# Rotary queries and keys kept transposed through DRAM, instead of turned by matrix products for each unit

## The chip, the cores and the metric

The kernel runs on one core of one Trainium2 chip. The metric is the device time of one execution in microseconds, the median of several runs. The core has TensorE (PE, matrix products), VectorE (DVE), ScalarE (ACT), GpSimd (POOL) and SyncE (SP), which issues most DMAs. Each engine takes its instructions in the order in which they were written.

## The reference

One layer on x of 4096 tokens by 256: attention, layer norm, a gated feed-forward network (FFN) of width 1024, layer norm. Cut to the part that the change touches:

```python
proj = quant4(x) @ ternary_weight(Wqkv_w).T + Wqkv_b
q = proj.reshape(B, N, h, dk).transpose(0, 2, 1, 3)   # 16 heads of 16 columns
k = proj.reshape(B, h, N, dk)                         # heads are blocks of 256 tokens
v = proj.reshape(B, h, N, dk)
q, k = (rotary(q, N), rotary(k, N))                   # even and odd columns turned by cos, sin
ql, kl = (q @ U, k @ U)
att = jnp.einsum('bhnr,bhmr->bhnm', ql, kl) / math.sqrt(dk)
y = jax.nn.softmax(att, axis=-1) @ v
```

`quant4` rounds each token to integers from -8 to 7 times the token's maximum over 7; `ternary_weight` makes the weight -1, 0 or 1 times a scale per input column of the product. Queries take a head from a column group of 16; keys and values take a head from 256 tokens, and a key's 4096 positions are (token of the 256) x (column group of 16).

## The kernel before

**Units.** The attention is 64 units: 8 pairs of heads times 8 blocks of 512 queries. A unit has 32 steps, a step is one loop turn. In a step, `largest` (L470, L478) multiplies 128 queries of the unit by 512 keys for two heads, each into a PSUM bank `ps`, and VectorE takes the maximum of each row; `weights` (L516, L524), 40 steps behind (`LAG`), forms the transposed scores minus the maximum by two products for each head and ScalarE takes the exponential; `values` (L538), 4 steps further behind and once in two steps, multiplies them by the values. The banks `ps` are three, shared by `largest` and everything else that TensorE makes beside it.

**Operands.** TensorE wants `kT` (128 x 4096) and `qT` (128 x 512) with the inner dimension on the partitions: 64 rows per head, being the keys' high part, low part, high, low, and the queries' high, high, low, low (a product of float32 numbers by parts). `gmat` is U times U transposed, over the root of 16, in blocks; only the keys are multiplied by it.

**Where they come from.** `projection_steps` makes, for each block of 512 tokens, the projection in token order (`v_all`). `key_steps` rotates a pair's keys in token order on GpSimd, turns them by eight products with the identity (L362), multiplies them by `gmat` (L368), splits them in parts (L377, L378), doubles these (L383) and turns the result by 32 products with the identity in eight groups (L394), each evacuated by ScalarE. It runs once per pair, over four units of the pair before. `query_steps` does the same for each unit's queries: six rotations on GpSimd (L330 to L335), two instructions that split (L432, L433), four products that turn them (L440), one evacuation (L447).

**The order** is written out by hand: `at(step, f)` puts f in the list of a step, and a step's list runs in the order of entry before that step's `weights`. All engines follow that order. Blocks 1 to 7 are projected at steps 32(b - 2) + 17 and on (block 1 in unit 0). The lists of the blocks are filled before the lists of the units.

**The maxima's way.** At the end of a unit VectorE reduces the maxima (L483). At the next unit's step 1 ScalarE rounds them (L490) and GpSimd subtracts (L491, `m_parts`); at step 3 VectorE transposes them (L497, `m_turned`); SP stores them to DRAM and loads them as `m_rows` (L502, L505); `weights` needs these from step 8 on.

Of the kernel before, what the change touches and what calls it, by code (L numbers as in the profile page):

```python
# [9 lines left out]
F32 = mybir.dt.float32  # L10
# [8 lines left out]
P = 128  # L19
# [18 lines left out]
def attn_ffn_kernel(  # L38
# [17 lines left out]
    cos: bass.AP,  # L56
    sin: bass.AP,
# [23 lines left out]
    y_dram = [dram.tile([QB, D], F32, name=f"y_dram{b}") for b in range(NQB)]  # L81
    flag = const.tile([1, 1], I32, name="flag")
# [9 lines left out]
    def ternary(w, wabs, neg, bank, sgn, alpha):  # L92

# [7 lines left out]
        nc.vector.tensor_scalar(alpha, ps[:, :D], 1.0 / D, None, ALU.mult)  # L101
# [7 lines left out]
        nc.vector.scalar_tensor_tensor(sgn, w, th, neg, ALU.is_ge, ALU.subtract)  # L109

    def linear_steps(src, sgn, bank, eng, evacuate):


        held = {}

        def measure():

            ma = stat.tile([P, BT], F32, name="ma")
            nc.vector.tensor_reduce(ma, src, AX.X, ALU.max, apply_absolute_value=True)  # L119
            nc.vector.tensor_scalar(ma, ma, 1e-6, None, ALU.max)  # L120
            held["ma7"] = stat.tile([P, BT], F32, name="ma7")
            nc.vector.tensor_scalar(held["ma7"], ma, 1.0 / 7.0, None, ALU.mult)
            held["rec"] = stat.tile([P, BT], F32, name="rec")
            nc.vector.reciprocal(held["rec"], ma)

        def integers():
            t = quantp.tile([P, BT, D], F32, name="qtmp")
            rec = held["rec"].unsqueeze(2).broadcast_to([P, BT, D])
            eng.tensor_tensor(t, src, rec, ALU.mult)
            eng.tensor_scalar(t, t, 7.0, ROUND, ALU.mult, ALU.add)  # L130
            eng.tensor_scalar(t, t, ROUND, -8.0, ALU.subtract, ALU.max)
            held["q"] = quantp.tile([P, BT, D], BF16, name="qint")
            eng.tensor_scalar(held["q"], t, 7.0, None, ALU.min)
# [9 lines left out]
        def project(i0):  # L143
            ps = bank([P, 512], F32)
            for i in range(i0, i0 + 2):
                for k in range(2):
                    nc.tensor.matmul(  # L147
                        ps[:, ts(i - i0, D)],
                        lhsT=held["qT"][:, k, i, :],
                        rhs=sgn[:, k, :],  # L150
                        start=(k == 0),
                        stop=(k == 1),
                    )
            for i in range(i0, i0 + 2):
                evacuate(i, ps[:, ts(i - i0, D)], held["ma7"][:, i : i + 1])

        return measure, integers, transposed, lambda: project(0), lambda: project(2)


# [51 lines left out]
    def front_steps(b, bank):  # L211
# [10 lines left out]
        first, *others = linear_steps(yb, sgn_o, bank, nc.vector, evacuate)  # L222

        def integers():
            first()
            others[0]()
# [4 lines left out]
            *others[1:],  # L231
# [6 lines left out]
    with ExitStack() as actx:  # L238
# [7 lines left out]
        cos_q = big.tile([P, NT, HALF], F32, name="cos_q")  # L246
        sin_q = big.tile([P, NT, HALF], F32, name="sin_q")
        cos_k = big.tile([P, 2, H, HALF], F32, name="cos_k")
        sin_k = big.tile([P, 2, H, HALF], F32, name="sin_k")
# [19 lines left out]

        def set_up():  # L270
# [7 lines left out]
            ut, ut8, mask = small[:32, :DK], small[:32, P : 2 * P], small[:, 2 * P : 3 * P]  # L278
            nc.sync.dma_start(out=ut, in_=uT)
            nc.sync.dma_start(out=mask, in_=blockmask)  # L280
            tables = ((cos, cos_q, cos_k), (sin, sin_q, sin_k))
            for src, _, tk in tables:
                nc.sync.dma_start(out=tk, in_=src.rearrange("(a p c) f -> p a c f", a=2, p=P))
            nc.sync.dma_start(out=bias_bc, in_=bqkv.partition_broadcast(P))
            for src, tq, _ in tables:
                nc.sync.dma_start(out=tq, in_=src.rearrange("(t p) f -> p t f", p=P))
# [3 lines left out]
            ternary(tw[0], wabs[:, 0], neg[:, 0], bank1, sgn_qkv, alpha_qkv)  # L290
            nc.gpsimd.tensor_copy(
                ut8.rearrange("r (j e) -> r j e", e=DK), ut.unsqueeze(1).broadcast_to([32, 8, DK])
            )
            psg = bank1([P, 512], F32)
            nc.tensor.matmul(psg[:, :P], lhsT=ut8, rhs=ut8, start=True, stop=True)
            nc.vector.tensor_tensor(gmat, psg[:, :P], mask, ALU.mult)

            def later():

                nc.gpsimd.memset(minus.bitcast(F32), -1.0)  # L300
                nc.gpsimd.memset(m_parts.bitcast(F32), 0.0)
                for i in range(2):
                    nc.gpsimd.memset(m_rows[i].bitcast(F32), 0.0)
                nc.gpsimd.memset(v_chunk[:, :, :, DK : DK + 1], 1.0)
                nc.gpsimd.memset(v_all[:, :, H * (DK + 1) :], 0.0)
                ternary(tw[1], wabs[:, 1], neg[:, 1], bank1, sgn_o, alpha_o)

            return later

        def projection_steps(b, eng):  # L310


            def evacuate(i, ps, ma7):
                v = v_chunk[:, b * BT + i, :, :DK]
                nc.vector.scalar_tensor_tensor(
                    v,
                    ps.rearrange("p (c e) -> p c e", e=DK),
                    ma7,
                    alpha_qkv.rearrange("p (c e) -> p c e", e=DK),
                    ALU.mult,  # L320
                    ALU.mult,
                )
                eng.tensor_tensor(v, v, bias_bc.rearrange("p (c e) -> p c e", e=DK), ALU.add)

            return linear_steps(x_bufs[b % 2], sgn_qkv, bank1, eng, evacuate)

        def rotate(lo, hi, even, odd, c, s, shape, key, eng=nc.gpsimd):

            t = [rot.tile(shape, F32, name=f"{key}{i}") for i in range(4)]
            eng.tensor_tensor(t[0], even, c, ALU.mult)  # L330
            eng.tensor_tensor(t[1], odd, s, ALU.mult)
            eng.tensor_tensor(lo, t[0], t[1], ALU.subtract)
            eng.tensor_tensor(t[2], even, s, ALU.mult)
            eng.tensor_tensor(t[3], odd, c, ALU.mult)
            eng.tensor_tensor(hi, t[2], t[3], ALU.add)  # L335

        def key_steps(pair, kT, eng=nc.gpsimd):


            kr = kprep.tile([P, 2, H, 2, DK], F32, name="kr")  # L340
            krT = kprep.tile([P, 2 * H * 2 * DK], F32, name="krT")
            kn = kprep.tile([P, 2 * H, 2, 4, DK], F32R, name="kn")

            def rotate_keys(j):
                src = v_chunk[:, 2 * (2 * pair + j) : 2 * (2 * pair + j) + 2]
                rotate(
                    kr[:, :, :, j, :HALF],
                    kr[:, :, :, j, HALF:],
                    src[:, :, :, 0:DK:2],
                    src[:, :, :, 1:DK:2],  # L350
                    cos_k,
                    sin_k,
                    [P, 2, H, HALF],
                    "rk",
                    eng,
                )

            def transpose_raw(i):
                ps = ps_1.tile([P, 512], F32, name="ps1")
                flat = kr.rearrange("p a c j e -> p (a c j e)")  # L360
                for k in range(4):
# [591 lines left out]
```

## Time and profile before

| what | value |
|---|---|
| median of 3 runs | 3701.32 us (3701.28 to 3702.39) |
| the profiled execution | 3702.95 us |
| its span | 3701.1 us, 62137 instructions |
| granted TensorE clock, mean | 0.986 |
| first L478 (VectorE) | 39.4 us |
| L483 of unit 0, 7, 63 | 96.1, 430.5, 2951.4 us |
| last `weights` product, FFN from | 3003 us, 3008 us |

The chain of waits follows the work that ended last back from the end, and gives each engine and line its share. A row of the timeline has start and length in us, engine, line, operation, tiles and shapes, and in brackets how long the engine was idle before it and for whom. A row of the groups has the busy time, the mean of one in ns, and the idle time before them. A row of the stretches has the busy time of PE, PEld, DVE, ACT and POOL with the count of instructions, the granted clock, the DMA share and GB/s.

### The profile page before, as it was taken

Reading aid. Unit: us, or ns where it says so; the run is one execution under the profiler, and the core shown is the slowest. Engines: PE = TensorE matmul, PEld = TensorE weight load, DVE = VectorE, ACT = ScalarE, POOL = GpSimd, SP = SyncE. Lnnn points to the kernel's source line nnn. Section 1 sums busy time; section 2 is a strip of 40 time slices with the busy share of each in tenths; the row PEclk is TensorE's granted clock in tenths of the full one; section 3 lists DMA queues with packets and bytes.
Section 4 is the critical chain, followed back from the end, with each engine's and each line's share of the span. In section 5 each row is a group of like instructions: output and inputs, shape, how many; then the busy total and the mean of one; then the engine's idle time right before and its main releaser. Section 6 shows DMA issues by size and latency. Waiting matters only on the chain.

```text
span 3701.1 us, 62137 instructions
## 1 busy us (share of the span) xinstructions
PE 3627.2 (98%) x24395; PEld 2055.8 (56%) x24395; DVE 3066.4 (83%) x5638; ACT 2384.5 (64%) x2782; POOL 525.0 (14%) x968
## 2 busy tenths in 40 slices
PE   6999999999999999999999999999999979999998
PEld 3454555555555555555555555555555448888887
DVE  6998999999999999998999899989999925555544
ACT  1567777777777777777777777777777753333333
POOL 3342112111211121121112111210111010000000
PEclk7999999999999999999999999999999989999999
DMA  1000000011000000000000000000121020001000
GB/s 37 15 24 14 20 20 20 20 23 23 20 20 20 20 20 20 21 20 20 20 20 20 20 20 20 20 14 14 38 64 26 21 82 6 18 18 35 18 6 13
DMA packets 247038, 84.52 MB, mean 23 GB/s; under 512 B 188880, under 2 KB 241360, under 8 KB 246736
## 3 DMA queue, kind: packets, MB, share of 16 engines
q1 hardware_dynamic: 242912, 68.93, 8.3%
q0 software_dynamic: 3824, 11.54, 1.0%
q8 instruction: 193, 3.16, 0.4%
q14 instruction: 109, 0.89, 0.1%
HBM read 54.22 MB, written 26.21 MB: 22 GB/s over the span
## 4 chain that ended last, share of the span: by engine, by line
PE 97%; DVE 2%; ACT 0%; DMA 0%; POOL 0%; issue 0%; SPq 0%; DVEq 0%; ACTq 0%; POOLq 0%
PE av L538 27%; PE sc L516 27%; PE ps L470 21%; PE ps_mm L785 17%; PE ps L394 1%; PE ps L440 1%; DVE mx L478 1%; PE ps L368 1%; PE ps L147 0%; DMA y_raw<-yt 0%; PE ps L362 0%; DVE ma L119 0%; PE ps_mm L830 0%; ACT pr L524 0%; PE ps_mm L147 0%
## 5 line engine op out<-in xcount | busy, mean ns | idle before, releaser
L478 DVE TENSOR_REDUCE mx<-ps 128x1 f32<-128x512 f32 x4096 | 2560.4, 684 | 210.7 <-PE ps L470 165.6
L524 ACT ACTIVATE pr<-sc 128x1024 f32<-128x1024 f32 x2048 | 2006.6, 1023 | 773.2 <-PE sc L516 759.4
L470 PEld LDWEIGHTS ps<-kT,qT 64*128 64x128 f32 x4096 | 557.7, 185 | 968.8 <-DVE mx L478 747.4
L538 PE MATMUL av<-pr,v_all 128*32 128x512 f32 x8192 | 1092.8, 605 | 0.0
L470 PE MATMUL ps<-kT,qT 64*128 64x512 f32 x4096 | 1051.7, 471 | 10.9 <-DVE mx L478 8.6
L516 PE MATMUL sc<-m_rows,minus 64*128 64x512 f32 x4096 | 842.7, 404 | 4.0 <-ACT pr L524 3.6
L516 PE MATMUL sc<-qT,kT 64*128 64x512 f32 x4096 | 817.7, 390 | 0.0
L516 PEld LDWEIGHTS sc<-m_rows,minus 64*128 64x128 f32 x4096 | 394.4, 185 | 89.1 <-ACT pr L524 38.3
L516 PEld LDWEIGHTS sc<-qT,kT 64*128 64x128 f32 x4096 | 395.7, 185 | 75.8
L538 PEld LDWEIGHTS av<-pr,v_all 128*32 128x32 f32 x8192 | 161.7, 108 | 267.3 <-issue 266.6
L818 ACT ACTIVATE gate<-ps_mm,sc_hs 128x512 f32<-128x512 f32 x128 | 88.3, 690 | 312.6 <-PE ps_mm L785 269.5
L491 POOL TENSOR_TENSOR m_parts<-m,m_parts 128x8 fp32r<-128x8 f32 x64 | 13.0, 203 | 1849.3 <-ACT m_parts L490 1849.3
L767 DVE CAST h<-gate 128x512 fp32r<-128x512 f32 x128 | 54.4, 425 | 223.1 <-ACT gate L818 223.0
L769 DVE TENSOR_TENSOR h<-gate,h 128x512 fp32r<-128x512 f32 x192 | 132.3, 689 | 5.1
L559 DVE STREAM_TRANSPOSE yt<-ya 128x64 f32<-128x64 f32 x512 | 119.0, 234 | 18.8 <-ACT ya L553 18.8
L785 PE MATMUL ps_mm<-h,h1a 128*128 128x512 f32 x512 | 128.9, 394 | 0.0
L785 PE MATMUL ps_mm<-h,h2a 128*128 128x512 f32 x512 | 127.2, 390 | 0.0
L785 PE MATMUL ps_mm<-h,h1b 128*128 128x512 f32 x512 | 126.5, 389 | 0.0
L785 PE MATMUL ps_mm<-h,h2b 128*128 128x512 f32 x512 | 126.5, 389 | 0.0
L810 DVE SCALAR_TENSOR_TENSOR gate<-ps_mm,sc_s,gate 128x512 f32<-128x512 f32 x64 | 48.0, 750 | 83.2 <-ACT gate L808 58.0
L785 PEld LDWEIGHTS ps_mm<-h,h1b 128*128 128x128 f32 x512 | 96.1, 188 | 20.1
L785 PEld LDWEIGHTS ps_mm<-h,h2b 128*128 128x128 f32 x512 | 96.1, 188 | 20.0
(147 smaller groups left out, 1954.1 us busy)
## 6 DMA issues: line engine op xcount, KB each, us to landing
y_raw<-yt SPq DMA_DIRECT2D x256, 64.0 KB
y<-y_raw SPq DMA_DIRECT2D x64, 256.0 KB
xs<-in_x SPq DMA_DIRECT2D x16, 512.0 KB
y_dram<-yu SPq DMA_DIRECT2D x64, 64.0 KB
xs<-in_h1T SPq DMA_DIRECT2D x8, 512.0 KB
xs<-in_h2T SPq DMA_DIRECT2D x8, 512.0 KB
yb<-y_dram SPq DMA_DIRECT2D x8, 512.0 KB
out<-xs SPq DMA_DIRECT2D x8, 512.0 KB
```

What stands on the lines that cost most here:

```text
L368: nc.tensor.matmul(ps[:, ts(k, P)], lhsT=krT[:, ts(4 * i + k, P)], rhs=gmat, start=True, stop=True,)
L470: nc.tensor.matmul(ps[j], lhsT=qTs[u][rows, ts(qt, P)], rhs=kTs[u // NQB][rows, ts(ck, 512)], start=True, stop=True,)
L478: nc.vector.tensor_reduce(mxs[u][:, qt, j, ck : ck + 1], ps[j], AX.X, ALU.max)
L516: nc.tensor.matmul(ps[:, j, :], lhsT=minus[rows, :] if first else kTs[u // NQB][rows, ts(kt, P)], rhs=m_rows[u % 2][rows, :] if first else ...
L524: nc.scalar.activation(pr, ps, AF.Exp)
L538: nc.tensor.matmul(avs[u][strip : strip + 32, :], lhsT=v_all[:, 2 * (2 * pair + j) + a, c * (DK + 1) : c * (DK + 1) + 32], rhs=probs[s + k ...
L559: nc.vector.transpose(yts[u][:, ts(i, 64)], yas[u][:, ts(i, 64)])
L767: eng(dst[:, k, 0, :], g)
L769: nc.vector.tensor_tensor(dst[:, k, 1, :], g, dst[:, k, 0, :].bitcast(F32), ALU.subtract)
L785: nc.tensor.matmul(ps, lhsT=sb[:, ks, ts(o, P)] if split else wo[:, k, :], rhs=src[:, k, i, :], start=(k == 0 and i == 0), stop=(k == n - ...
L810: nc.vector.scalar_tensor_tensor(g, pb, scales["s2"][:, o : o + 1], gate, ALU.mult, ALU.mult)
L818: nc.scalar.activation(g, ps, AF.Gelu, scale=scales[sc][:, o : o + 1])
```

## The change

Queries and keys are no longer taken from the projection in token order. For each block of 512 tokens the projection is made a second time, transposed: the weight's even columns and then its odd columns are the stationary operand, so that row (column group, frequency) x token comes out (`even_odd`). There the rotation is a plain product with tables `csq` (for queries) and `csk` (for keys) of the same layout. The token's scale, which was a scalar per partition, is now a row: `start_scales` stores the maxima to DRAM and loads them to all partitions. `queries` rotates, splits in high and low and `store_queries` writes them to `q_dram`. `rotate_keys` rotates with the other table, `regroup_keys` moves halves of 64 partitions by DMA so that a head's 16 rows stand together, `times_g` multiplies by `gmat` (two products of 512 columns) and splits, `store_keys` writes to `k_dram`. A unit's `qT` is loaded by four DMAs (`load_queries`), a pair's `kT` by eight (`load_keys`). `key_steps`, `query_steps` and `rotate` are gone, with L362, L368, L394 and L440. The positions of the keys are in another order (`values` takes c and a the other way round).

Block b, from 1 to 7, is now worked wholly within unit b - 1 and the start of unit b, since its queries are the ones of unit b. For blocks from 1 on GpSimd does the even and odd rows' scale and bias, the rotations, the parts of the queries and the natural projection's scale and bias, and ScalarE empties the banks; for block 0, before the first step, VectorE and ScalarE do most of it. The zero and one fills and the output weight's signs, which stood at step 8, stand before the first step. Two scalar operations of the rounding have another form. The diff, cut:

```diff
-            nc.vector.tensor_scalar(ma, ma, 1e-6, None, ALU.max)
+            eng.tensor_scalar(ma, ma, 1e-6, None, ALU.max)
...
-            eng.tensor_scalar(t, t, ROUND, -8.0, ALU.subtract, ALU.max)
+            eng.tensor_scalar(t, t, 1.0, -ROUND, ALU.mult, ALU.add)
...
-            eng.tensor_scalar(held["q"], t, 7.0, None, ALU.min)
+            eng.tensor_scalar(held["q"], t, 7.0, -8.0, ALU.min, ALU.max)
...
+        def start_scales(b, held):
+            row = ma_dram[b % 2]
+            nc.sync.dma_start(out=row.rearrange("t p -> p t"), in_=held["ma7"])
+            held["scale"] = rot.tile([P, QB], F32, name="scale")
+            nc.sync.dma_start(out=held["scale"],
+                in_=row.rearrange("t p -> (t p)").unsqueeze(0).broadcast_to([P, QB]))
+        def even_odd(b, held, o):
...
+            for k in range(2):
+                nc.tensor.matmul(ps, lhsT=sgn_qkv[:, k, o::2],
+                    rhs=held["qT"][:, k].rearrange("p t q -> p (t q)"),
+                    start=(k == 0), stop=(k == 1))
+            if b:
+                nc.scalar.activation(x, ps, AF.Copy, scale=alpha2[:, o : o + 1])
+                nc.gpsimd.tensor_tensor(x, x, held["scale"], ALU.mult)
+                nc.gpsimd.tensor_scalar(x, x, bias2_sb[:, o : o + 1], None, ALU.add)
...
+        def queries(b, held):
+            t, u = two("rot")
+            copies, second = (nc.gpsimd.tensor_copy, nc.gpsimd) if b else (nc.scalar.copy, nc.vector)
+            c, s = (held["cs"][:, i].unsqueeze(1).broadcast_to([P, 2, QB]) for i in range(2))
+            nc.gpsimd.tensor_tensor(t, held["eo"], c, ALU.mult)
+            nc.gpsimd.tensor_tensor(u, held["eo"], s, ALU.mult)
+            nc.gpsimd.tensor_tensor(t[:, 0], t[:, 0], u[:, 1], ALU.subtract)
+            second.tensor_tensor(u[:, 0], u[:, 0], t[:, 1], ALU.add)
...
+            for h, x, eng in ((0, t[:, 0], nc.gpsimd), (1, u[:, 0], second)):
+                copies(q[:, h, 0], x)
+                eng.tensor_tensor(q[:, h, 1], x, q[:, h, 0].bitcast(F32), ALU.subtract)
...
+        def rotate_keys(b, held, eng):
...
+            eng.tensor_tensor(t.rearrange(by_head, j=2), eo, c, ALU.mult)
+            eng.tensor_tensor(u.rearrange(by_head, j=2), eo, s, ALU.mult)
+            eng.tensor_tensor(t[:, 0], t[:, 0], u[:, 1], ALU.subtract)
+            eng.tensor_tensor(u[:, 0], u[:, 0], t[:, 1], ALU.add)
...
+        def times_g(b, held, x):
+            ps = bank1([P, QB], F32)
+            nc.tensor.matmul(ps, lhsT=gmat, rhs=held["keys"][:, x], start=True, stop=True)
+            high, low = (held["parts"][:, 2 + x, i] for i in range(2))
+            nc.scalar.copy(high, ps)
+            nc.vector.tensor_tensor(low, ps, high.bitcast(F32), ALU.subtract)
...
+        def load_queries(u, queue=nc.sync):
+            pair, qb = divmod(u, NQB)
+            qTs[u] = qpool.tile([P, QB], F32R, name="qT", bufs=3)
+            for j in range(2):
+                for i in range(2):
+                    row = 64 * j + 2 * DK * i
+                    queue.dma_start(out=qTs[u][row : row + 2 * DK, :].bitcast(F32),
+                        in_=q_dram[qb][2 * pair + j, i].unsqueeze(0).broadcast_to([2, DK, QB]))
...
             for b in range(1, NQB):
-                steps = projection_steps(b, nc.gpsimd)
-                first = NKT * (b - 2) + 16 if b > 1 else 0
+                first = NKT * (b - 1)
...
+                    for i in range(BT):
+                        at(first - 9 + 2 * i, lambda i=i, f=biggest: f(i))
...
+                def prepare(b=b, h=h, measure=measure, integers=integers):
+                    measure()
+                    start_scales(b, h)
+                    h["cs"] = load_tables(b)
+                    integers()
+                if b > 1:
+                    at(first + 1, prepare)
...
+                at(first + 10, transposed)
+                for o in range(2):
+                    at(first + 12 + 2 * o, lambda b=b, h=h, o=o: even_odd(b, h, o))
+                at(first + 15, lambda b=b, h=h: queries(b, h))
+                at(first + 23, lambda b=b, h=h: store_queries(b, h))
+                for i in range(2):
+                    at(first + 16 + 2 * i, lambda b=b, h=h, i=i: natural(b, h, 2 * i))
+                at(first + 22, lambda b=b, h=h: rotate_keys(b, h, nc.gpsimd))
+                at(first + 34, lambda h=h: regroup_keys(h))
+                for x in range(2):
+                    at(first + 39 + 2 * x, lambda b=b, h=h, x=x: times_g(b, h, x))
+                    at(first + 43, lambda b=b, h=h, x=x: store_keys(b, h, x))
...
-                        steps = key_steps(pair + 1, kTs[pair + 1])
-                        for i, f in enumerate(steps):
-                            at(NKT * u + 40 + 6 * i, f)
+                        for i in range(4):
+                            at(NKT * u + 40 + 8 * i,
+                                lambda i=i: load_keys(pair + 1, kTs[pair + 1], i // 2, i % 2))
...
-                    at(NKT * (u - 1) + 26 if u else 0, transposed)
...
-                    at(NKT * (u - 1) + (18 if u == 1 else 6), start_queries)
+                    at(NKT * (u - 1) + (25 if u < NQB else 14), lambda u=u: load_queries(u))
```

## The prediction

> **What bounds the kernel now.** I read the page's busy times and its chain of waits first.
>
> ```profile
> PE 3627.2 (98%) x24395; PEld 2055.8 (56%) x24395; DVE 3066.4 (83%) x5638; ACT 2384.5 (64%) x2782; POOL 525.0 (14%) x968
> ...
> PE av L538 27%; PE sc L516 27%; PE ps L470 21%; PE ps_mm L785 17%; PE ps L394 1%; PE ps L440 1%; DVE mx L478 1%; PE ps L368 1%; PE ps L147 0%; DMA y_raw<-yt 0%; PE ps L362 0%; DVE ma L119 0%; PE ps_mm L830 0%; ACT pr L524 0%; PE ps_mm L147 0%
> ```
>
> TensorE is the chain. The lines that the change deletes (L394, L440, L362; L368 is replaced by as much) are in it, so they are paid for. By how much, the timeline of VectorE in the last units tells: L483 runs once per unit, and the last unit has no query turn (L440) for a successor.
>
> ```profile
> 2864.12 0.22 DVE L483 TENSOR_REDUCE m<-mx 128x8 f32<-128x64 f32 x1
> ...
> 2908.09 0.22 DVE L483 TENSOR_REDUCE m<-mx 128x8 f32<-128x64 f32 x1
> ...
> 2951.39 0.22 DVE L483 TENSOR_REDUCE m<-mx 128x8 f32<-128x64 f32 x1
> ```
>
> 43.97 us with L440, 43.30 without: 0.67 us a unit. The timeline of all engines in unit 8 says the same: `av` bursts are 2.70 us apart, but 3.38 across L440.
>
> ```profile
> 462.82 1.06 PE L538 MATMUL av<-pr,v_all 128*32 128x512 f32 x8
> ...
> 464.71 0.66 PE L440 MATMUL ps<-identr,qq 128*128 128x128 f32 x4
> ...
> 466.20 1.06 PE L538 MATMUL av<-pr,v_all 128*32 128x512 f32 x8
> ```
>
> The table by stretches (PE, PEld, DVE, ACT, POOL busy) shows a plain unit and a cycle of eight with one key preparation:
>
> ```profile
> 460.10:504.20 44.10, 44.07 (x325) 22.25 (x324) 41.50 (x76) 33.27 (x40) 3.95 (x11) 1.00 0.08 15
> ...
> 697.70:1059.10 361.40, 361.34 (x2654) 184.11 (x2654) 333.93 (x602) 267.93 (x309) 55.81 (x110) 1.00 0.10 21
> ```
>
> 361.4 - 8 x 44.03 = 9.2 us per pair for L362, L368 and L394; from the gaps between bursts, 2 x 0.68 + 2 x 1.17 + 8 x 0.68 = 9.1. VectorE (41.5 of 44.1) is next, 1.8 us short of the 43.3 that remain: it does not take over in a plain unit.
>
> **Steady part, units 8 to 63.** 56 x 0.67 = 37.5 us and six key preparations (pairs 2 to 7), 6 x 9.2 = 55.2 us, go: **-92.7 us**. What comes in their place is on SP and the DMA engines: 4 query loads per unit and 8 key loads (256 KB each) per pair. They are issued 18 or more steps (24 us) before use; w1's 1 MB took 6.6 us to land. The last key pair is issued 3 steps before `m_turned`'s store; that hop takes 2.0 us (rows below), and `m_rows` is read 5 steps (6.8 us) after it, so some 2.8 us cover it. Without cover: at most about 3 us x 7.
>
> **The first eight units pay.** Before, L483 of units 0 and 7 are at 96.1 and 430.5: 334.4 us for seven units, 31.3 above 7 x 43.3. Now six of those units (1 to 6) each do a whole block on GpSimd. What its instructions cost, by groups and by the timeline of GpSimd:
>
> ```profile
> L620 POOL TENSOR_TENSOR xs<-xs,wround 128x1024 f32<-128x1024 f32 x22 | 52.4, 2383 | 1.8
> ...
> L330 POOL TENSOR_TENSOR rk<-v_all,cos_k 128x256 f32<-128x256 f32 x14 | 10.4, 746 | 0.0
> ...
> L383 POOL CAST kn<-kn 128x1024 fp32r<-128x1024 f32 x14 | 14.5, 1042 | 0.1
> ```
> ```profile
> 266.41 1.89 POOL L129 TENSOR_TENSOR qtmp<-xs,rec 128x1024 f32<-128x1024 f32 x1 [13.39 <-DVE rec L124]
> 268.39 1.05 POOL L130 TENSOR_SCALAR qtmp<-qtmp 128x1024 f32<-128x1024 f32 x1
> 269.52 3.64 POOL L131 TENSOR_SCALAR qtmp<-qtmp 128x1024 f32<-128x1024 f32 x1
> 273.24 2.77 POOL L133 TENSOR_SCALAR qint<-qtmp 128x1024 bf16<-128x1024 f32 x1
> ```
>
> A two-input operation: 2.38 us at 1024, 0.74 at 256, so 1.29 at 512. Multiply-then-add (L130) is fast, the forms with subtract, max or min are slow. Per block:
> - integers: 1.89 + 1.05 + 1.05 (the subtraction is now a multiply-add) + the new min-then-max. That form is not in the trace: 2.77 (one operation) to 6.4 (3.64 + 2.77); I take 3.64, the two-operation row. Sum 7.6.
> - even and odd rows: 2 x (1.29 + adding a bias by pointer). The latter, at 512: 0.5 (half of L130) to 1.8 (half of L131); I take 1.4, half of the single operation L133. Sum 5.4.
> - queries: 4 products and sums, 2 x 2.38 + 2 x 1.29, 2 casts of 0.6, 2 subtractions of 1.29: 11.1.
> - natural: 4 x (0.74 + 0.68) = 5.7; rotated keys: 2 x 2.38 + 2 x 1.29 = 7.3.
>
> 37.1 us, with the small ones (limits, `m_parts`, y, yu) 38.6, of a unit of 44: it fits, but in a poor order. `prepare` (first + 1) and `largest_parts` stand at the same step and `prepare` was entered first; GpSimd runs the four integer operations, then the small L491. Before, this chain was, by the timeline:
>
> ```profile
> 475.76 0.20 POOL L491 TENSOR_TENSOR m_parts<-m,m_parts 128x8 fp32r<-128x8 f32 x1 [27.76 <-ACT m_parts L490]
> ...
> 478.41 0.20 DVE L497 STREAM_TRANSPOSE m_turned<-m_parts 128x32 f32<-128x32 f32 x1
> 478.64 0.53 SPq L502 DMA_DIRECT2D m_dram<-m_turned  x1
> ...
> 480.62 0.57 SPq L505 DMA_DIRECT2D m_rows<-m_dram  x2
> ```
>
> Two steps (2.7 us) lie between the reciprocal and `m_turned`; now 7.6 + 0.3 of gaps + 0.2 = 8.2 us must pass. VectorE stands some 5.5 us with all reductions behind it, the three `ps` banks fill, and TensorE stops at its next L470, after perhaps 1 us of cover. If more covers it: rival 1. On SP, ahead of `m_turned`'s store, now stand three issues of `prepare` with one hop of 2.0 us and four of the regrouping at 0.5: done by R + 5, inside the 8.2.
>
> **How long a unit then is.** Let R be the reciprocal. `m_turned` at R + 8.2; to step 12, 9 steps x 1.35 + 0.7 (transposes) = 12.9; two matmuls and ScalarE's evacuation 1.8: R + 22.9. GpSimd has waited for that. Even 2.7; odd is there at R + 26.3 and done at 29.0; queries 40.1, natural 45.8, keys 53.1. `prepare` comes next in its queue; with 1 us of gaps (0.08 between rows) the next R is near R + 54. TensorE by itself: 43.3 + transposes 0.77, even and odd 1.25 (as many columns as natural), natural 2 x 0.63, two products by gmat 2.34 (as L368's two groups) = 48.9, plus the stop of 4.5: 53.4. The two nearly agree; ScalarE's additions (2 x 0.6, 4 x 0.45, 2 x 0.6) and VectorE's (about 3.3) lie beside this. I take **54 us** for units 1 to 6 and 46 for unit 7 (only gmat's products): 370 against 334.4, **+35.6 us** (the unknown rows reach from -1.7 - 0.9 to +0.8 + 2.8 a unit, some -15 to +22 in all).
>
> Queries' stores wait on SP for R + 40 (behind them on SP: the query loads, and the gather of `y_raw` at step 29, whose reader has a unit of time), land by about R + 45 (1 MB in 2 to 6.6 us), the loads by R + 49, and the first L470 of the next unit comes near R + 52. That holds narrowly; each us more is a us of stall.
>
> **Start.** Before: VectorE's first L478 at 39.39, L483 at 96.1. Now, serial from x (about 4.7): maximum 1.2, limits 0.5, integers 3.3 (12.66 to 16.1 before), transposes, copy and even/odd 5, evacuation 2.3, rotation by 4 VectorE operations 3.8: 21. Regrouping by DMA 3.5, gmat 2 x 2, split 1.3, stores to 32; loads of 2 MB on two queues, ScalarE's behind the queries' store and load: 43; `output_weights` and VectorE's 3.3 us of it and of x's maximum: 47. Unit 0 then has no L394: 32 x 1.2 (18 reductions took 10.83) + 5.2 of TensorE at its half clock + about 6 of turns between banks and VectorE's maxima = 50. **97 against 96: +1** (-5 to +15: three DMA hops of 2.0 to 6.6 each).
>
> **Sum.** Execution of the profile 3702.95 (span 3701.1): -92.7 + 35.6 + 1 = -56 gives 3647. The three runs' median is 1.6 lower: **3645**. FFN and tail are unchanged: their edits are the same VectorE forms (0.69 each) under matmuls.
>
> **Two rules weighed.** PE's clock was 0.50 in the stretch from 40 to 108 us, and 0.54 in 3010 to 3020, inside a wait of 16.25 us; after waits of 1.0 to 1.1 us (120, 167, 215) it stayed 1.00. The Trainium skill, "TensorE: Matmul & The Clock Gate", section "Why this matters for your kernels", warns of idle gaps over some 3 us: "One MID window of idle → back to K=4/8". The stops forecast here are 4.5 us; by the rule some of the six would add an estimated 2 to 3 us each, up to 15 in all. By the rows shown, that is open.
>
> Each query load here is written as 2 copies of 16 rows. The page "DMA: Bandwidth & Descriptors", in "Why a DMA increments its semaphore by 16 and not by 1", says a DMA uses as many engines (up to 16) as divide both slowest dimensions: 2 here. At its 27 GiB/s an engine, an estimated 4.5 us for the four loads; no row of before shows such a load. By it the queries would be 2 us late in units 1 to 6: 12 us more.
>
> **Rivals.**
> 1. *The stop is hidden*: GpSimd's min/max is quick and TensorE sets the pace, 48.9 a unit. 6 x 48.9 + 45.7 = 339: +5 + 1 - 92.7 = **3614**. Against it: the order of GpSimd's queue.
> 2. *VectorE takes over in the steady units, or loads are late*: if units stay at 44.0 instead of 43.3, 37 us of gain are gone: **3682**. For it: VectorE is 94% busy. Against it: the last unit's 43.30 with the same reductions.
> 3. *Slower*: GpSimd overruns the unit. If its operations took 1.4 times the rows (38.6 to 54), R to R grows by 13, six times: +78, **3723**. It turns to a loss from about 9.5 us more a unit (1.25 times). For it: GpSimd goes from 16 to 39 us in these units, nearly without a pause. Against it: the rows were taken beside the same reductions.
> 4. *It does not do what it says*: excluded for the products, since L362, L394 and L440 have no successors after unit 7.
>
> **Chances.** Forecast (3628 to 3665) 0.58; rival 1 (under 3628) 0.17; rival 2 or a longer start (3665 to 3694) 0.11; within 0.2% (3694 to 3709, about what a measurement here can tell from no change) 0.04; rival 3 0.10. Faster 0.86. The range of 8 in 10 is 3612 to 3690.
>
> **What would show it.** Right: L483's successor 43.3 us apart from unit 8; in units 1 to 6 a wait of the `m_turned` transpose for GpSimd's `m_parts` of some 5 us, and 52 to 56 us a unit. Wrong: steady units at 44; `ps` waiting for the DMA of `qT` at unit starts by over 2 us; first reduction after 60 us.

## The result, and the profile after

The changed kernel takes **3732.09 us** (median of four runs, 3728.62 to 3732.47) against 3701.3 (3700.27 to 3702.39) for the kernel before on the same chip: a ratio of 1.0081, 95% interval 1.0064 to 1.0099. It is slower by 0.8%; the forecast was 3645. The profiled execution took 3732.24, its span is 3730.5, so 29.4 us more than before. The page first: busy times and the two rows of the chain.

```profile
PE 3561.5 (95%) x23756; PEld 1995.5 (53%) x23763; DVE 3053.7 (82%) x5607; ACT 2328.8 (62%) x2682; POOL 435.0 (12%) x521
...
PE 90%; DMA 5%; POOL 3%; DVE 1%; SPq 0%; issue 0%; ACT 0%; ACTq 0%; DVEq 0%; POOLq 0%
PE av L588 26%; PE sc L566 25%; PE ps L520 20%; PE ps_mm L866 17%; DMA ma_dram<-ma 1%; DMA keys<-rot 1%; PE ps L447 1%; DVE mx L528 1%; DMA y_raw<-yt 0%; DMA q_dram<-qk 0%; POOL qk L410 0%; POOL v_all L497 0%; POOL v_all L494 0%; POOL rot L429 0%; DMA kT<-k_dram 0%
```

TensorE has 66 us less to do, as it should; but it is no longer the whole chain. DMA and GpSimd now hold 8% of it, and the two DMAs named first are new ones: the store of the scales (`ma_dram`, L363) and the regrouping of the keys (`keys`, L439). The successor of L483, L533, shows where the time went. Timeline of VectorE, start of the instruction first, at the ends of units 0, 1, 2, 7, 8 and 63:

```profile
116.20 0.22 DVE L533 TENSOR_REDUCE m<-mx 128x8 f32<-128x64 f32 x1
180.45 0.22 DVE L533 TENSOR_REDUCE m<-mx 128x8 f32<-128x64 f32 x1
244.01 0.22 DVE L533 TENSOR_REDUCE m<-mx 128x8 f32<-128x64 f32 x1
...
550.78 0.22 DVE L533 TENSOR_REDUCE m<-mx 128x8 f32<-128x64 f32 x1
594.17 0.22 DVE L533 TENSOR_REDUCE m<-mx 128x8 f32<-128x64 f32 x1
...
2979.91 0.22 DVE L533 TENSOR_REDUCE m<-mx 128x8 f32<-128x64 f32 x1
```

| stretch | before | forecast | after | after - before |
|---|---|---|---|---|
| start to L533 of unit 0 | 96.1 | 97 | 116.2 | +20.1 |
| units 1 to 7 | 334.4 | 370 | 434.6 | +100.2 |
| units 8 to 63 | 2520.9 | 2428.2 | 2429.1 | -91.8 |
| behind it | 749.7 | 749.7 | 750.6 | +0.9 |

The gain is there, almost to the microsecond; the first units and the start ate it. What TensorE waited for between 116 and 551 us (line waited at, what released it, us in total, times, longest):

```profile
PE ps L447 <- DMA keys<-rot: 54.8, 6, 11.7
PE ps L520 <- DVE mx L528: 15.8, 8, 3.3
PE ps L520 <- DMA qT<-q_dram: 2.7, 3, 1.7
PE ps L520 <- ACT qT L157: 0.5, 1, 0.5
```

The second row is the stop that the forecast named. The first, over three times as large, it did not name: TensorE stands at gmat's product (`times_g`) once in each of units 1 to 6, until the regrouped keys land. Timeline of SP in one of them (start, duration, what is issued):

```profile
246.12 0.38 SPq L363 DMA_DIRECT2D ma_dram<-ma  x1
255.09 0.34 SPq L365 DMA_DIRECT2D scale<-ma_dram  x1
255.48 0.62 SPq L294 DMA_DIRECT2D cs_q<-in_csq  x1
256.15 3.85 SPq L439 DMA_DIRECT2D keys<-rot  x4
260.10 0.62 SPq L552 DMA_DIRECT2D m_dram<-m_turned  x1
266.02 0.57 SPq L555 DMA_DIRECT2D m_rows<-m_dram  x2
```

SP issues the store of the scales, must load them back, and so stands **9 us** for the landing of 2 KB. All that is behind it in SP's order is late: the 512 KB of `cs_q`, the regrouping, and `m_dram`. The regrouping's source had been finished by GpSimd at 245.46, by its timeline:

```profile
244.18 1.28 POOL L431 TENSOR_TENSOR rot<-rot,rot 128x512 f32<-128x512 f32 x1
```

Timeline of TensorE in the same place:

```profile
256.73 0.40 PE L520 MATMUL ps<-kT,qT 64*128 64x512 f32 x2
265.34 2.05 PE L447 MATMUL ps<-keys,gmat 128*128 128x512 f32 x2 [8.20 <-DMA keys<-rot]
267.31 1.94 PE L588 MATMUL av<-pr,v_all 128*32 128x512 f32 x8
```

And the table by stretches of that unit: length, busy TensorE, weight loads, VectorE, ScalarE and GpSimd, granted clock, DMA share, GB/s:

```profile
249.70:252.50 2.80, 0.00 (x1) 0.00 (x0) 0.84 (x3) 1.35 (x2) 2.20 (x4) 1.00 0.00 0
252.50:254.00 1.50, 1.50 (x5) 0.46 (x9) 1.50 (x3) 0.00 (x0) 0.00 (x0) 0.52 0.00 0
...
265.30:269.00 3.70, 3.66 (x10) 0.70 (x10) 0.80 (x2) 0.58 (x1) 0.08 (x1) 0.50 0.02 3
```

Behind each stop, the 2.8 us at `m_turned` (249.70 to 252.50) and the 8.2 at the keys, TensorE runs at half its clock for a few microseconds.

### The profile page after: what moved, and what is told of

The parts are those of the page before. It is cut to its first block, busy times and chain, and to the rows that moved or that the text cites. A ratio compares the mean times of both kernels' runs of the same rounds, so it can differ in the third digit from the quotient of the medians.

```text
span 3730.5 us, 60927 instructions
## 1 busy us (share of the span) xinstructions
PE 3561.5 (95%) x23756; PEld 1995.5 (53%) x23763; DVE 3053.7 (82%) x5607; ACT 2328.8 (62%) x2682; POOL 435.0 (12%) x521
## 4 chain that ended last, share of the span: by engine, by line
PE 90%; DMA 5%; POOL 3%; DVE 1%; SPq 0%; issue 0%; ACT 0%; ACTq 0%; DVEq 0%; POOLq 0%
PE av L588 26%; PE sc L566 25%; PE ps L520 20%; PE ps_mm L866 17%; DMA ma_dram<-ma 1%; DMA keys<-rot 1%; PE ps L447 1%; DVE mx L528 1%; DMA y_raw<-yt 0%; DMA q_dram<-qk 0%; POOL qk L410 0%; POOL v_all L497 0%; POOL v_all L494 0%; POOL rot L429 0%; DMA kT<-k_dram 0%
## 5 line engine op out<-in xcount | busy, mean ns | idle before, releaser
L528 DVE TENSOR_REDUCE mx<-ps 128x1 f32<-128x512 f32 x4096 | 2550.8, 683 | 151.3 <-PE ps L520 100.2
L520 PEld LDWEIGHTS ps<-kT,qT 64*128 64x128 f32 x4096 | 567.0, 186 | 1001.2 <-DVE mx L528 858.1
L520 PE MATMUL ps<-kT,qT 64*128 64x512 f32 x4096 | 1065.0, 475 | 23.9 <-DVE mx L528 17.3
L566 PE MATMUL sc<-m_rows,minus 64*128 64x512 f32 x4096 | 826.4, 398 | 5.1 <-ACT pr L574 3.0
L866 PEld LDWEIGHTS ps_mm<-h,h1b 128*128 128x128 f32 x512 | 96.1, 188 | 20.1
L866 PEld LDWEIGHTS ps_mm<-h,h2b 128*128 128x128 f32 x512 | 96.1, 188 | 19.9
```

Source lines behind the costliest of these rows:

```text
L520: nc.tensor.matmul(ps[j], lhsT=qTs[u][rows, ts(qt, P)], rhs=kTs[u // NQB][rows, ts(ck, 512)], start=True, stop=True,)
L528: nc.vector.tensor_reduce(mxs[u][:, qt, j, ck : ck + 1], ps[j], AX.X, ALU.max)
L566: nc.tensor.matmul(ps[:, j, :], lhsT=minus[rows, :] if first else kTs[u // NQB][rows, ts(kt, P)], rhs=m_rows[u % 2][rows, :] if first else ...
L866: nc.tensor.matmul(ps, lhsT=sb[:, ks, ts(o, P)] if split else wo[:, k, :], rhs=src[:, k, i, :], start=(k == 0 and i == 0), stop=(k == n - ...
```

## The experiments

Theory S: SP's wait for the scales' store makes the keys late, and TensorE, which works in order, loses the time at `times_g`. Rivals: GpSimd's pace (G), the regrouping DMA itself or the load ahead of it (D, Q), the stop at `m_turned` (M), a landing that takes as long whatever the pieces are (P), narrow query loads (K); at the start, ScalarE's queue (A) or the keys' loads (L). Times are medians, "m0" is L533's successor in unit 0, "units" the mean of units 1 to 6; the changed kernel has 3732.1, 116.2 and 64.8.

| run | us | m0 | units | ratio to before (95%) |
|---|---|---|---|---|
| e1_late_scale | 3671.7 | 117.4 | 55.3 | 0.9904 to 0.9937 |
| e2_row_store | 3667.8 | 108.7 | 55.4 | 0.9895 to 0.9928 |
| e3_parts_first | 3727.1 | 116.9 | 63.8 | 1.0054 to 1.0088 |
| e5_late_tables | 3705.3 | 117.6 | 60.4 | 1.0002 to 1.0021 |
| e4_split_queries | 3716.3 | 112.8 | 63.3 | 1.0028 to 1.0062 |
| e6_abs_early | 3722.6 | 115.3 | 63.3 | 1.0046 to 1.0079 |
| e8_units | 3640.6 | 108.9 | 51.0 | 0.9819 to 0.9852 |
| e9_units_start | 3640.4 | 110.1 | 50.6 | 0.9822 to 0.9855 |
| e10_best | 3632.0 | 104.8 | 50.3 | 0.9796 to 0.9829 |
| e12_long_rows | 3636.9 | 109.2 | 50.5 | 0.9809 to 0.9842 |
| c1_after_again | 3730.7 | 117.8 | 64.5 | 1.006 to 1.0093 |

### The order on SP alone (e1_late_scale)

```diff
                 def prepare(b=b, h=h, measure=measure, integers=integers):
                     measure()
-                    start_scales(b, h)
-                    h["cs"] = load_tables(b)
+                    store_scales(b, h)
                     integers()
+                def fetch(b=b, h=h):
+                    scales_back(b, h)
+                    h["cs"] = load_tables(b)
...
+                at(first + 8, fetch)
```

> Only the order on SP changes in units 1 to 6: the store of the scales stays at step first + 1, and the load back of the scales and the load of cs_q move to step first + 8, behind the regrouping and m_dram. Theory S (SP stands 9 us for the landing of the scales' store, with the regrouping and m_dram behind it, and TensorE then stands 8 to 12 us in front of times_g): the regrouping is issued some 9 us earlier, the wait of TensorE for keys goes (54.8 us over six units), units 1 to 6 take 54 to 57 us instead of 64.8, 3665 to 3680 us in all. Rival G (GpSimd's 38 us of operations and their order set the pace of these units): units stay at 62 or more, 3715 to 3735. Rival D (the regrouping DMA itself lands too late, 5 steps after its issue): some 4 us a unit stay, about 3700.

60 us gained, by order alone: the load back and the load of `cs_q` behind it in the queue stand seven steps later. Timeline of SP in the same unit:

```profile
228.26 0.37 SPq L364 DMA_DIRECT2D ma_dram<-ma  x1
228.73 2.46 SPq L444 DMA_DIRECT2D keys<-rot  x4
```

The regrouping now follows the store by 0.5 us, not 10, and TensorE's waits for keys in units 1 to 6 fell from 54.8 us to 2.9:

```profile
PE ps L452 <- DMA keys<-rot: 2.9, 2, 2.3
```

G, which had 62 or more for the units, falls, and D, which had some 4 us a unit left, too.

### The same order, a cheaper store (e2_row_store)

```diff
+            nc.vector.transpose(ma_turned, ma_pad[b % 2])
             row = ma_dram[b % 2]
-            nc.sync.dma_start(out=row.rearrange("t p -> p t"), in_=held["ma7"])
+            nc.sync.dma_start(out=row.rearrange("r (b c) -> b r c", b=4), in_=ma_turned)
...
```

The tiles are also widened to 32 columns for the transpose.

> Order kept; the scales are turned by a 32x32 transpose on VectorE and stored as 128 pieces of 128 bytes instead of 512 pieces of 4 bytes. Theory S: the store lands in some 2 us as m_dram's does, not 9; all that stands behind it on SP is 7 us earlier, in units 1 to 6 and at the start; TensorE's wait for keys falls from 9 to about 2 us, and the first reduction comes some 5 us earlier: 3675 to 3690. Rival P (the landing takes 9 us whatever the pieces are, because of where it lies in the queue or because of DRAM): 3728 to 3738. Rival G: the start gains 5 us, the units nothing: 3725.

```profile
220.61 0.58 SPq L371 DMA_DIRECT2D ma_dram<-ma_turned  x1
222.60 0.35 SPq L373 DMA_DIRECT2D scale<-ma_dram  x1
223.00 0.62 SPq L301 DMA_DIRECT2D cs_q<-in_csq  x1
223.72 2.55 SPq L447 DMA_DIRECT2D keys<-rot  x4
```

SP stands 2.0 us instead of 9.0 (timeline of SP), and TensorE's waits for keys fell to 6.6 us, 5.9 of them in one unit:

```profile
PE ps L455 <- DMA keys<-rot: 6.6, 3, 5.9
```

The run is 7 us better than its range: the start gained 7.5 us instead of 5, and the clock in the units rose with the shorter waits (0.97 and 1.00 in units 2 and 3, where it was 0.89). P falls. Two independent cures of one wait give the same units, 55.3 and 55.4: S holds.

### The forecast's own stop taken away (e3_parts_first)

```diff
-                    integers()
                 if b > 1:
                     at(first + 1, prepare)
+                    at(first + 2, integers)
```

> Only GpSimd's order changes: the four integer operations move from step first + 1 to first + 2, behind m_parts, so the stop of m_turned that the forecast named (2.8 us a unit, 16.9 in six) goes. Theory S: TensorE comes 2.8 us earlier to times_g and stands there 2.8 us longer, since the keys hang on SP's wait; no gain, 3725 to 3735. Rival M (the stop at m_turned is what costs, as the forecast had it): 17 us or more are gained, 3710 to 3716.

The wait at `m_turned` is gone, and what TensorE waits for is:

```profile
PE ps L447 <- DMA keys<-rot: 70.9, 6, 12.9
PE ps L520 <- DMA qT<-q_dram: 1.9, 1, 1.9
PE ps L520 <- DVE mx L528: 1.4, 2, 1.0
```

14.4 us less in the row of `mx`, 16.1 more in that of the keys: whoever comes earlier to a late transfer only waits longer. M falls. (The 5 us that the run is faster are not shown to come from the edit: e6_abs_early below, which leaves the units alone, is 9.5 us faster.)

### Only the 512 KB out of the way (e5_late_tables)

```diff
                     start_scales(b, h)
-                    h["cs"] = load_tables(b)
                     integers()
+                def fetch(b=b, h=h):
+                    h["cs"] = load_tables(b)
...
+                at(first + 8, fetch)
```

> Only the load of cs_q (512 KB) moves from step first + 1 to first + 8, behind the regrouping; the scales' store and load stay in front of it. Theory S: the regrouping is still issued 9 us late, but finds the queue empty; it lands perhaps 4 to 5 us earlier than now: a half of the wait stays, 3700 to 3712. Rival Q (the 512 KB in front of the regrouping in the queue are the cause, not the store): as much as in the run with the late scales, 3665 to 3680.

```profile
PE ps L447 <- DMA keys<-rot: 28.8, 6, 8.5
```

28.8 us of the wait for keys stay, 26 go: the load of `cs_q` ahead of the regrouping is about half of the damage, but only because SP's wait has made all of them late together; in e2 it still stands ahead, and 6.6 us are left. Q alone falls.

### Narrow query loads (e4_split_queries)

```diff
-                    row = 64 * j + 2 * DK * i
-                    queue.dma_start(out=qTs[u][row : row + 2 * DK, :].bitcast(F32),
-                        in_=q_dram[qb][2 * pair + j, i].unsqueeze(0).broadcast_to([2, DK, QB]))
+                    for c in range(2):
+                        row = 64 * j + DK * (2 * i + c)
+                        queue.dma_start(out=qTs[u][row : row + DK, :].bitcast(F32),
+                            in_=q_dram[qb][2 * pair + j, i])
```

> Each query load of two copies of 16 rows becomes two loads of 16 rows (8 issues a unit instead of 4), all else as in the changed kernel. Theory S: TensorE waited for these loads twice and 1.7 us at most in the first units, and the keys' wait follows in the same unit: 3727 to 3735. Rival K (the copies as the slowest dimension hold each load to two DMA engines, so the queries are late by some 2 us in each unit): 3716 to 3724.

S's number was missed. K's range holds the result, but not by K's mechanism: 16 us less, of it 3.4 at the start, 9.4 in units 1 to 7 and 3.0 behind, and TensorE's waits for queries in these units, which K had at 12 us, were 2.7 in the changed kernel. It was the wait for keys that fell, from 54.8 to 44.0. In a steady unit the 128 packets of the four loads lie over 6.0 us (1126.45 to 1132.44), never more than 4 at a time; those of the eight loads over 2.9 us (1158.40 to 1161.32), up to 16 at a time. So the form with two copies in front is slow, as the Trainium skill, "DMA: Bandwidth & Descriptors", section "Why a DMA increments its semaphore by 16 and not by 1", has it (engines by a common divisor of the slowest dimensions: 2 here); the forecast had set the 12 us estimated from that page aside, and they did not come in these units. The units' part is not cleanly the split's own: the next run shows nearly the same without it. Nor is the part behind them: that stretch, 750.6 us in the changed kernel, took 752.0 when it was run again (c1) and 748 in e11, both without the split.

### Output weights earlier (e6_abs_early, e9_units_start)

```diff
             queries(0, held)
+            output_weights()
...
                 natural(0, held, 2 * i)
-            output_weights()
```

> Only the start changes: the absolute values, sums and signs of the output weights come ahead of gmat's products and of ScalarE's DMA issues, not behind them. Theory A (ScalarE's absolute value stands behind twelve DMA issues of its own queue until 65.2 us, and TensorE's first products of unit 0 behind that): the first reductions come 3 to 5 us earlier, 3726 to 3730. Rival L (the keys' loads, 2 MB in 16 DMAs until 65 to 68 us, bound the start in any case): 3730 to 3734, and TensorE waits for kT instead.

In the changed kernel TensorE stands from 43.99 to 65.84 before the output weights' product, for a ScalarE instruction behind twelve DMA issues. With that out of the way it stands from 43.94 to 64.03 for `kT`. m0 gained 0.9 us: L is right, the loads bound the start. The kernel got 9.5 us faster all the same, outside both ranges, nearly all of it in units 1 to 6, where the scales' store landed in 8.6 us on the mean instead of 9.5: 0.9 of the 1.5 us gained per unit. The changed kernel was run once more to see whether that was chance.

> The changed kernel once more, beside the other three kernels of this call, as their base. In the last call two kernels that leave the units alone had units 1 to 6 shorter by 9 us in all, with the scales' store landing in 8.0 to 8.3 us in most units where it had been 8.6 to 9.4. If the landing of that store differs from one placement of a run to another, this run shows it too: 3718 to 3733, and its units shorter or longer by as much as the six landings are.

It repeats itself: 3730.7 us, units of 64.5, landings of 9.6 on the mean. So the shorter landing seems to go with the kernel and not with the execution; why is open. Where units wait for that store, differences of up to some 9 us are therefore not put down to an edit by the time alone.

> The run of the three cures of the units, and at the start the output weights ahead of gmat's products and unit 0's keys loaded by 8 DMAs of 256 KB instead of 16 of 128 KB. Theory A with S: 4 to 9 us less than the run without the change at the start, 3624 to 3636. Rival L: the start stays within 2 us.

This run adds the same move, and unit 0's keys in 8 loads of 256 KB instead of 16, to e8_units, the next one here: 0.2 us apart from it. L again.

### All three cures of the units (e8_units)

The edits of e2 and e3, and `scales_back` with `load_tables` at first + 7.

> The scales stored as 128 pieces of 128 bytes, their load back and that of cs_q at step first + 7, and the integers behind m_parts, together. Theory S: both waits of TensorE (keys 9 us, m_turned 2.8 us a unit) go, no clock is lost, and units 1 to 6 take what TensorE has to do in them at full clock, 49.3 us in the units of the row-store run: 50 to 51.5 us each; about 3630 to 3642 in all. Rival G (GpSimd's chain from one reciprocal to the next then sets the pace): units stay at 53 to 55, 3655 to 3668.

Table by stretches, columns as before, units 2, 3 and 5:

```profile
160.43:210.97 50.54, 49.30 (x347) 23.36 (x345) 44.22 (x83) 36.28 (x44) 35.29 (x32) 1.00 0.32 90
210.97:261.15 50.18, 49.06 (x342) 23.05 (x335) 44.33 (x83) 36.28 (x44) 35.84 (x34) 1.00 0.59 126
...
314.35:364.77 50.42, 49.43 (x348) 23.59 (x353) 44.53 (x83) 36.28 (x44) 35.82 (x34) 1.00 0.35 97
```

against the changed kernel's units 2, 3 and 5:

```profile
180.45:244.01 63.56, 52.14 (x347) 23.90 (x345) 44.07 (x81) 36.29 (x44) 35.20 (x32) 0.89 0.25 71
244.01:308.51 64.50, 52.94 (x342) 23.87 (x336) 44.15 (x82) 36.28 (x44) 35.77 (x34) 0.89 0.46 98
...
375.94:441.08 65.14, 53.22 (x348) 24.65 (x353) 44.45 (x83) 36.18 (x44) 35.72 (x34) 0.90 0.32 75
```

The same work takes TensorE 49.3 us at full clock and 52.9 (mean of units 2 to 6) with the clock lost behind the stops; the units shown are within 1.3 us of that (unit 4, 53.2, still waits 2.0 for queries; unit 1 begins on the start's low clock). GpSimd has the same 35.2 to 35.8 us in both, and does not pace them.

### The best version (e10_best), and the start (e12_long_rows)

e8 with e4's split loads:

> The three cures of the units, and each query load as two loads of 16 rows. The units wait for queries 2.9 us in all without the split, the start gained 3.4 us by it: 3632 to 3637 if the split was worth only that; 3624 to 3630 if the 13 us less of the split alone in the first call were its own.

3632.0 us: faster than both kernels, 1.9% under the one before. The split is worth 8.6 us here, 4.1 at the start and 3.9 in the units, where the clock stays at 1.00.

> As the run with the three cures and the split loads, and the keys in DRAM laid with each row's 4096 elements together, so that a load reads 16 KB rows and not 1 KB pieces (the stores, 8 of 128 KB instead of 4 of 256 KB per block, keep 1 KB pieces). Theory B (the keys' loads of unit 0 are bound by their 1 KB pieces: in a steady unit six such loads ran at 113 GB/s with the DMA engines over 90% busy, so 2 MB take 18 us where the forecast had 11): the first reduction comes 5 to 9 us earlier, 4 to 9 us less in all than the run without it. Rival W (the loads wait for the stores' landing and for semaphores, not for bytes): within 2 us.

```diff
-    k_dram = [dram.tile([2, 2, H, DK, N // H], F32, name=f"k_dram{b}") for b in range(NQB)]
+    k_dram = [dram.tile([2, 2, DK, H, N // H], F32, name=f"k_dram{b}") for b in range(NQB)]
```

4.9 us more instead of less, 4.4 of them at the start, so W's 2 us are missed as well. The keys' loads ran at about 137 GB/s with 8 KB packets as they did at 133 with 1 KB (e10), and the stores, now in eight DMAs, ended later. B falls as written: the loads are slow, not because of short pieces.

### The store by itself (e11_piece_sizes, e13_quiet_sizes)

> The changed kernel and in units 36 to 53 one more store and a load back of it on SP, of zeros that nothing reads, in six forms by turns: 512 pieces of 4 bytes (the scales' form), 128 pieces of 4 bytes, 128 of 16 bytes, 128 of 128 bytes, 512 of 4 bytes that lie 512 bytes apart, and one of 2 KB. Measured is the time from the store's issue to that of the load that waits for it. Theory S1 (each 4-byte piece is paid at its place in DRAM, so the number of pieces counts): some 9, 3 to 4, 3, 2, 9 and 2 us. Theory S2 (pieces that fall in the same line of DRAM wait for one another): 9, 3 to 4, 3, 2, but the pieces that lie apart land in 2 to 3 us. The kernel as a whole: 3720 to 3733.

This run (3730.0 us) told less than meant: SP runs ahead of the steps, so each trial store was issued 0.6 us behind the query loads and stood behind their packets; even one piece of 2 KB took 5.4 to 5.6 us. The forms that lie side by side in 4 bytes took 9.3 to 13.0, the ones 512 bytes apart 5.8 to 6.4; of the others one trial, of 128-byte pieces, took 12.7. So it was done again with a tile that VectorE clears at the step, which holds SP back.

> The changed kernel, and in units 20 to 46 one more small transfer each on SP, in nine forms by turns, three times each, now begun only when VectorE has cleared its tile at step 22 of the unit, so that no query load stands in the queues before it. Stores of zeros that nothing reads, then a load back that waits: 512 pieces of 4 bytes side by side (the scales' form), 128 of 4 bytes side by side, 128 of 16 bytes, 128 of 128 bytes, 512 of 4 bytes lying 512 bytes apart, one of 2 KB. Theory S2 (4-byte pieces that share a line of DRAM wait for one another): the first two 6 to 9 us, all others 2 to 2.5 us. Theory S1 (the number of pieces counts): the first and the fifth 6 to 9, the second 3, the others 2 to 2.5. And loads of 2 KB rows, then a store that waits: four of 16 rows, eight of 16 rows, one of 128 rows. If loads into 16 partitions are bound by the partitions, the eight take clearly longer than the one of 128 rows beyond their issue (8 x 0.4 us); if not, they take about 2 us after the last issue, as the one does. The kernel as a whole: 3722 to 3735.

What SP waited for (total, times, longest), of the run's waits of SP; a to f are the forms in the order of the expectation, a, b, e, d, c and f in the rows:

```profile
SPq L694 <- DMA try_a<-try_src: 27.1, 3, 10.3
SPq L694 <- DMA try_b<-try_src: 22.7, 3, 8.4
...
SPq L694 <- DMA try_e<-try_src: 4.4, 3, 1.5
SPq L694 <- DMA try_d<-try_src: 3.3, 3, 1.2
...
SPq L694 <- DMA try_c<-try_src: 3.1, 3, 1.1
...
SPq L694 <- DMA try_f<-try_big: 2.6, 3, 0.9
```

From issue to issue: 512 pieces of 4 bytes side by side 8.8 to 10.7 us, 128 of them 7.4 to 8.9; the same 512 pieces 512 bytes apart 2.1; 128 pieces of 16 bytes 1.4 to 1.5, of 128 bytes 1.5 to 1.7; one of 2 KB 1.2. It is not the number of pieces, nor the bytes: 4-byte pieces side by side in DRAM are what is slow. S2 named the right forms as slow and as quick (the first ran past its 9 us, most quick ones came under 2); its reason is not shown, since pieces of 16 bytes, also neighbours, pay nothing. As to the loads, eight of 16 rows landed 2.0 us behind the last issue, one of 128 rows after 2.7 us, so no brake by the 16 partitions shows. But the eight were issued 0.46 us apart, 32 KB each, which is some 70 GB/s: a brake at 133 GB/s could not have shown. Why unit 0's keys came at 133 GB/s stays open. (The kernel as a whole took 3741.8, above its range: the trials held up a few steady units, one by 6.3 us.)

## Why the prediction was wrong, step by step

- **Steady units: right.** -91.8 against -92.7. Units 8 to 63 are 43.38 apart on the mean (43.2 in the last eleven); VectorE did not take over, and of the loads only `m_rows` was late, once, by 0.6 us.
- **SP's order in units 1 to 6: the step that failed.** The forecast had, of SP, "three issues of `prepare` with one hop of 2.0 us", and all "done by R + 5". With R the reciprocal at 245.81, the load of the scales was issued at R + 9.3 and `m_dram` at R + 14.3. The hop of 2.0 us was read from `m_dram`, a store in 128-byte pieces, and given to one in 4-byte pieces, of which no row existed; it took 9.0. It should have had bounds, like the min/max. And the forecast asked only whether `m_dram` was held up. The regrouping stands in the same queue, and its reader, `times_g`, five steps on, stands in TensorE's order: it was costed as work (2.34 us) and never as a wait. That wait was 9.1 us a unit on the mean.
- **The stop at `m_turned`: mechanism right, size too large.** 5.5 us on VectorE were forecast, 4.5 on TensorE; it was 2.6 to 3.3 on VectorE and 2.1 to 3.3 on TensorE (in unit 4, 1.0 on VectorE). The term that was mis-sized is the min-then-max, by the timeline of GpSimd:

```profile
249.18 1.04 POOL L147 TENSOR_SCALAR qtmp<-qtmp 128x1024 f32<-128x1024 f32 x1
250.31 1.04 POOL L149 TENSOR_SCALAR qint<-qtmp 128x1024 bf16<-128x1024 f32 x1
251.43 0.20 POOL L541 TENSOR_TENSOR m_parts<-m,m_parts 128x8 fp32r<-128x8 f32 x1
```

  1.04 us, not 3.64, and below the range of 2.77 to 6.4: these two operations in one instruction cost what the multiply-add in the row above costs. The bias by pointer took 1.57 (1.4 forecast); the other rows held.
- **TensorE's own part: right.** 48.9 us forecast, 49.3 measured at full clock.
- **The clock: a cost set aside.** Before, stops of 1.1 us kept the clock; here it is halved behind 2.80 us (0.52 in the next 1.5 us), and so it is with the 8.2. It costs 52.9 - 49.3 = 3.6 us a unit, some 18 in units 2 to 6; unit 1, which begins on the start's low clock, has the same 49.47 us of TensorE in the changed kernel and in e8. The estimate worked out in the prediction from the Trainium skill, "TensorE: Matmul & The Clock Gate", section "Why this matters for your kernels", was 2 to 3 a stop; the gap of some 3 us that it starts from is too long here. Behind a gap of 1.70 us in unit 4 (308.31 to 310.01) the clock was already 0.50, from 310.60 to 314.00; in e1, behind 1.38 us (280.13 to 281.51), it stayed 1.00 for the next 3.4. In a unit of 64.9 (mean of 2 to 6) then: 49.3 work, 3.6 clock, 12.0 waits. The forecast's 54 had 48.9 and 4.5. Some 10.8 us more in each of six units (64.8 for 54) are the 65 us by which units 1 to 7 were missed.
- **The start: +20 for +1.** The first product of unit 0 stands at 67.85 us; its reduction was forecast for 47. By the same product in the runs (59.94 in e2, 60.14 in e8, 56.04 in e10), 7.9 of the 20.9 are the scales' store, 4.1 the narrow query loads. Another 5.2 are the keys' rotation on VectorE, 9.0 us for 3.8 forecast; that is read from the timeline, and no run takes it away. In e2, timelines of VectorE and GpSimd:

```profile
18.25 1.23 DVE L436 TENSOR_TENSOR rk<-eo,cs_k 128x1024 f32<-128x1024 f32 x1
19.39 3.36 DVE L437 TENSOR_TENSOR rk<-eo,cs_k 128x1024 f32<-128x1024 f32 x1
22.79 2.79 DVE L438 TENSOR_TENSOR rk<-rk 128x512 f32<-128x512 f32 x1
...
18.30 3.37 POOL L410 TENSOR_TENSOR rot<-eo,cs_q 128x1024 f32<-128x1024 f32 x1 [9.55 <-DVE eo L400]
21.63 3.39 POOL L411 TENSOR_TENSOR rot<-eo,cs_q 128x1024 f32<-128x1024 f32 x1
```

  The first product takes 1.23, the equal second 3.36: it ends 1.1 us after GpSimd's product of 18.30 to 21.67 does, and GpSimd's next starts at 21.63. They take turns. That agrees with the Trainium skill, "SBUF — State Buffer", section "SBUF: two separate sides", which has an exclusive lock between the two engines for such pairs. The last 3.7 us are what is left over. A likely place, not shown by a run, is the loads of 2 MB, which the forecast priced by w1's load (1 MB in 6.6 us, some 160 GB/s) and which ran at 133 GB/s in e10.
- **Rivals.** The slower side came, but not by GpSimd: 38.6 us of operations were 35.2 to 35.8, and in e10 units take 50.3 with the same GpSimd work. Rival 1's unit of 48.9 (3614) is near what the cures reach (50.3, 3632).
- **Signs named.** `m_turned` waiting for `m_parts` showed, and a larger wait, which no sign had named, came behind it; "first reduction after 60 us" was named as wrong, and came.

## What to carry to other kernels

Price a DMA by its pieces, from a row of the same form, and if there is none, give it bounds as for an instruction; then walk down the queue behind the waiting issue and ask of each transfer which in-order engine reads it next and when. Work that is cheap on an idle engine can still cost its whole queue: here 2 KB cost 60 us through SP's order, and either moving the load that waits for the store seven steps later or storing rows turned a loss of 0.8% into a gain of 0.8 or 0.9%. And where two waits lie in one unit, take both away before judging either: the smaller one alone gave 5 us of 3732 at most, both together, with a quiet clock and 7 us of it at the start, 91.

## What the hardware showed that was not expected

- 4-byte stores side by side to DRAM: 7.4 to 10.7 us from issue until SP goes on, the same pieces 512 bytes apart 2.1, 16-byte pieces 1.4. In unit 1 the store was issued at 118.95, its 512 packets had all been taken up by 120.22, and SP was let go at 127.92: the wait lies behind the packets.
- Behind gaps of 2.80 and 1.70 us on TensorE its clock was halved; behind gaps of 1.38 us (e1) and 1.1 (before) it was not.
- GpSimd's min-then-max by two constants on 128 x 1024: 1.04 us, against 2.77 for the min alone and 3.64 for subtract-then-max in the kernel before.
